# Moved steps in SyncE's queue and in a K block's reads: a graph layer and an attention layer on one core

## The chip, the cores and the metric

The kernel runs on one core of a Trainium2 chip. The metric is the device time of the whole kernel in microseconds (us). Before the change the median of three runs is 2260.26 us (2256.02 to 2264.42).

## The reference

The input x has 128 batch elements of 128 nodes with 512 features, in float32; adj is one 128x128 matrix for all of them.

```python
# layer 0
h = relu(layernorm(x))
x = x + norm_adj @ (h @ W0) + b0          # norm_adj = D^-1/2 adj D^-1/2
# layer 1: attention over the nodes, 8 heads of 64
h = relu(layernorm(x))
q, k, v = h @ Wq + bq, h @ Wk + bk, h @ Wv + bv
s = q k^T / sqrt(64) + (1 - adj) * -1e9
x = x + softmax(s) v @ Wo + bo
```

## The kernel before

**Tiles and stages.** The batch is cut into 32 groups of four elements (NG = 32, GB = 4). A group's x lies in SBUF as two tiles `xt`, half 0 (elements 0 and 1) and half 1 (elements 2 and 3), 512 KB each. The layers are pipelined over groups: in iteration t of the main loop the blocks run in the order W, Q, K, V, Y. W is the product with W0 for group t+1, Q, K and V are the projections for group t, Y is the output projection of group t-1. One iteration takes about 69 us.

**A projection** (class `Projection`) is one 512x512x512 product done as seven products of blocks P1 to P7, in the order P1, P5, P2, P6, P3, P7, P4, one for each step n = 0 to 6. P5, P2, P3 and P4 are again cut into seven products of smaller blocks each (`seven`, `phase`). TensorE writes them into PSUM banks: P1, P6, P7 in one of two banks a (they take turns between projections), P5 and P3 in d0 and d1, P2 in b, P4 in c. VectorE adds the pieces of a bank to the output tile (`add`, L440, and `read`, L455); the first read of each part is ScalarE's in Q, K and V. `step(n)` records the matmuls and the reads that go with them, `rest(n)` further reads of the same step. In K alone, `whole` is set: there P4 is computed in steps 4, 5 and 6 of its own block, ScalarE copies its first pieces (`part`, L768), and VectorE adds the others. In all other blocks the second and third phase of P4 are the `tail`, done in steps 1 and 2 of the next block.

In K's step 4, `rest` records seven reads: two of bank_d1 (`read_three`), one of bank_b, then four of bank_d0: `read_columns`, `read_across` column 0, `read_minus`, `read_across` column 1. Step 5 then records the read of bank_c that follows P4's second phase, and two of bank a. Step 6 writes P4's third phase into bank_c.

**Order.** Each engine runs its instructions in the order of the program. `plan` holds what else is put between the steps: `at(t, "W3", f, ...)` calls f before step 3 of block W of iteration t (with a letter b or c, after the step's first or second part). Within one slot the order is that of the calls of `at`. The program's order is then the order in each engine's queue. SyncE (SP) issues all DMAs, so an issue that has to wait holds up all that follow.

**What SyncE does around the change**, with g = t - 1 the group whose attention is being finished:
- `split_att(g, b)` (L848, L849): ScalarE splits element b's attention weights into two planes of 16 bits, and a DMA writes these to DRAM (`planes`).
- `turn_att(g, b)` (L852): a transposing DMA brings the planes back, transposed, into the tile `att`. `attend` (L874) then uses them at the start of V, in the order of elements 2, 3, 0, 1; in the program the results of 2 and 3 go to banks named `po`.
- `store_half(t - 2, 1)` (L892): the finished half 1 of group t - 2 goes out. Half 0 goes out at the end of the Y block before.
- `load_x(t + 2, (half,))` (L170): the x tiles of group t + 2. They take the buffers of group t - 2, so each load waits until the store of the same half has landed.
- `reload_w` (L1058): weights, in four parts per projection, from copies in DRAM (`wd_q` and so on) into two buffers in turn.

`ln1` (L325, L326, L330) takes the statistics of the new x on VectorE: half 0's first element in slot Q0b, its second in Q1b, half 1 in Q3b. The reads of W's tail from bank_c stand behind the first of these on VectorE.

Of the kernel before, what the change touches and what calls it, by code (L numbers as in the profile page):

```python
# [97 lines left out]
def kernel(  # L98
# [177 lines left out]


    INNER = [((T1, W22), step) for step in FIRST_RIGHT[:3]]
    INNER += [((W21, T4), WINOGRAD_RIGHT[0])]
    INNER += [((T1, W22), step) for step in FIRST_RIGHT[3:]]  # L280
    INNER += [((W21, T4), step) for step in WINOGRAD_RIGHT[1:]]

    def combine_inner(name, engine, steps=range(9)):
# [103 lines left out]
    class Projection:  # L387
# [110 lines left out]
        def read_phase(self, half, y, src, n, part=(0, 1)):  # L498
# [8 lines left out]
            else:  # L507
                self.add(dst[:, 1], m[:, 1:2].to_broadcast([P, 2, P]))

        def step(self, n):  # L510

            a, inner = bank[f"a{turn[0]}"], self.inner
            t, m = self.region(1, 0), bank["c"]
            left = tail.pop(0) if n in (1, 2) and tail else None
            if n == 0:
                self.left, self.right = self.a(), w_sb[self.w]
                self.product(a, P1, True)
                self.read_first(0, 0, a)
            elif n == 1:
                if inner:  # L520
                    self.seven(P5, True, (0,))
                else:
                    self.product(bank["d0"], P5, True)
                if left:
                    left[0]()
                if inner:
                    self.seven(P5, True, (1,))
            elif n == 2:
                if inner:
                    self.phase(bank["b"], P2, 0)  # L530
                else:
                    self.product(bank["b"], P2, True)
                if left:
                    left[0]()
            elif n == 3:
                self.product(a, P6, False)
                self.read_first(0, 1, a)
            elif n == 4:
                if inner:
                    self.phase(bank["b"], P2, 1)  # L540
                    if self.whole:
                        self.phase(m, P4, 0)
                    self.seven(P3, False, (1, 0))
                    self.read_phase(0, 0, bank["b"], 1, (0,))
                    if self.whole:

                        self.whole(t[:, 0, :], m[:, P : 3 * P], 0)
                        self.whole(t[:, 1, P:], m[:, 3 * P :], 1)
                        self.add(t[:, 0, :P], m[:, :P])
                else:  # L550
                    self.product(bank["d0"], P3, False)
            elif n == 5 and self.whole:
                self.phase(m, P4, 1)
                self.product(a, P7, False)
                self.whole(t[:, 1, :P], m[:, 3 * P :], 1)
                self.add(t[:, 1, :P], m[:, P : 2 * P])
                self.add(t[:, 0, :], a[:, : 2 * P])
                self.add(t[:, 1, P:], a[:, 3 * P :])
                turn[0] = 1 - turn[0]
            elif n == 5:  # L560
                self.product(a, P7, False)

                reads = [lambda: self.read_first(1, 0, a), lambda: self.read(1, 1, a)]
                for f in reads if self.stay else reads[::-1]:
                    f()
                turn[0] = 1 - turn[0]
            elif self.whole:
                self.phase(bank["b"], P2, 2)
                self.phase(m, P4, 2)
                self.read_phase(0, 0, bank["b"], 2)  # L570
                a = bank[f"a{1 - turn[0]}"]
                self.add(t[:, 1, :P], a[:, 2 * P : 3 * P])
                self.read(1, 1, a)
                self.read_phase(1, 0, m, 2)
            elif inner:
                self.phase(bank["b"], P2, 2)
                self.phase(bank["c"], P4, 0)
                self.read_phase(0, 0, bank["b"], 2)
                self.read_phase(1, 0, bank["c"], 0)
                for k in (1, 2):  # L580
                    tail.append(
                        (
                            lambda k=k: self.phase(bank["c"], P4, k),
                            lambda k=k: self.read_phase(1, 0, bank["c"], k),
                        )
                    )
            else:
                self.product(bank["c"], P4, True)
                self.read(1, 0, bank["c"])
            if n == 2:  # L590
                if inner:
                    self.read_phase(0, 0, bank["b"], 0)
                else:
                    self.read(0, 0, bank["b"])
            if left:
                left[1]()

        def rest(self, n):

            inner = self.inner  # L600
            if n == 1:
                if inner:
                    self.read_columns(1, 1, True)
                else:
                    self.read_first(1, 1, bank["d0"])
            elif n == 2 and inner:
                self.read_three(1, 1, 0)
                self.read_across(1, 1, 0)
                self.read_three(1, 1, 1)
                self.read_across(1, 1, 1)  # L610
                self.read_minus(1, 1)
            elif n == 4:
                if inner:
                    self.read_three(0, 1, 0)
                    self.read_phase(0, 0, bank["b"], 1, (1,))
                    self.read_three(0, 1, 1)
                    self.read_columns(0, 1)
                    self.read_across(0, 1, 0)
                    self.read_minus(0, 1)
                    self.read_across(0, 1, 1)  # L620
                else:
                    self.read(0, 1, bank["d0"])

# [170 lines left out]
    def turned_in_place(g, b):  # L794

        return g == NG - 1 or (g, b) in ((0, 2), (0, 3), (NG - 2, 3))
# [102 lines left out]
    def at(slot, place, f, *args):  # L899
        plan.setdefault((slot, place), []).append((f, *args))  # L900

    for t in range(-1, NG + 1):
# [3 lines left out]
        if 0 <= t - 1 < NG - 1:  # L906
            g = t - 1

            for first, final, place, f, *args in (
                ("W1", "-Y6", "Q0", turn_att, 0),  # L910
                ("W4b", "-Y6b", "W1b", split_att, 1),
                ("W5", "-Y3", "W2", exponentials, 2, 0, H // 2),
                ("W6", "-Y4", "W3", exponentials, 2, H // 2, H),
                ("Q0b", "-Y5b", "W4b", softmax_end, 2),
                ("Q1", "-Y5", "W5", exponentials, 3, 0, H // 2),
                ("Q2", "-Y6", "W6", exponentials, 3, H // 2, H),
                ("Q0", "Q1", "Q2", turn_att, 1),
                ("Q2b", "Q0b", "Q0b", softmax_end, 3),
                ("Q4b", "Q0b", "Q3b", split_att, 2),
                ("Q6b", "Q2", "Q5b", split_att, 3),  # L920
                ("K1", "Q2", "K0", turn_att, 2),
                ("K3", "Q5", "K2", turn_att, 3),
            ):
                place = first if t == 1 else final if last else place
                if f in (split_att, turn_att) and turned_in_place(g, args[0]):
                    continue
                at(t - place.startswith("-"), place.strip("-"), f, g, *args)
            if t == 1:
                at(1, "K3", transpose_att, g, 2)
                at(1, "K5", transpose_att, g, 3)  # L930
            elif last:
                at(t, "K1", transpose_att, g, 3)
            for b in (2, 3, 0, 1):
                at(t, "V0", attend, g, b)
# [35 lines left out]

            at(t, "Y3" if t == NG else "Q3" if last else "W3", store_half, t - 2, 1)
        if 3 <= t + 2 < NG:
            at(t, "W3" if t > 1 else "W0", load_x, t + 2, (0,))
            at(t, "W5" if t > 1 else "W0", load_x, t + 2, (1,))
        if 2 <= t + 2 < NG:
            g = t + 2
# [255 lines left out]
```

## Time and profile before

| what | value |
|---|---|
| median of three runs | 2260.26 us |
| profiled execution: its own time | 2266.76 us |
| its span | 2265.0 us |
| TensorE busy | 2231.4 us (99%) |
| VectorE busy | 1799.0 us (79%) |
| ScalarE busy | 1385.6 us (61%) |
| GpSimd busy | 1867.5 us (82%) |
| DMA, hardware queue of SyncE | 560.08 MB, 84.7% of 16 engines |
| granted TensorE clock | 0.999 |

The profile is one execution; its span runs from the first to the last instruction, and its own time lies some 6.5 us over the median of the runs. Times in a timeline are us from the start of the span: start, duration, engine, line, operation, tiles written and read, count; a number in brackets is the idle time of the engine just before, with what ended it. PE is TensorE, PEld its weight loads, DVE VectorE, ACT ScalarE, POOL GpSimd, SP SyncE, and a q behind a name its sequencer. A line of waits names who waited for whom, the total in us, the number of times and the longest. A DMA is told of twice: the time SyncE needs to issue it, and the time from issue to landing. L is the line in the kernel before.

### The profile page before, as it was taken

What the parts mean: (1) busy time and instruction counts of PE and PEld (TensorE: products, weight loads), DVE (VectorE), ACT (ScalarE), POOL (GpSimd) and SP (SyncE); (2) the same over time, 40 slices, a digit from 0 to 9 for tenths busy, and PEclk for the clock granted to TensorE, in tenths of its full rate; (3) what the DMA queues carried; (4) which work ended last, traced back from release to release, by engine and by line L of the source; (5) the groups of instructions that cost most, each with busy time, mean ns of one, the idle gap of its engine ahead of it and who ended that gap; (6) DMA issues with size and microseconds to landing.
All of it is one profiled execution on the core that took longest, in us unless ns stands there. A gap on an engine that the chain in (4) does not pass through costs nothing.

```text
span 2265.0 us, 79243 instructions
## 1 busy us (share of the span) xinstructions
PE 2231.4 (99%) x32679; PEld 1903.6 (84%) x32679; DVE 1799.0 (79%) x4371; ACT 1385.6 (61%) x3556; POOL 1867.5 (82%) x1928
## 2 busy tenths in 40 slices
PE   9999999999999999999999999999999999999999
PEld 7688888888888888888888888888888888888887
DVE  7778887877888778878778877788777887877876
ACT  4565665655666556666556665566665665655754
POOL 6899888888898888898888988888888888878864
PEclk9999999999999999999999999999999999999999
DMA  5478988899888899888898899998898988899982
GB/s 172 158 261 252 282 237 268 248 251 287 252 259 251 248 266 266 276 255 246 259 287 246 258 243 252 273 258 265 249 246 260 287 247 260 247 248 280 246 240 96
DMA packets 448697, 565.15 MB, mean 250 GB/s; under 512 B 326352, under 2 KB 333648, under 8 KB 447824
## 3 DMA queue, kind: packets, MB, share of 16 engines
q1 hardware_dynamic: 448336, 560.08, 84.7%
q8 instruction: 258, 4.23, 0.7%
q14 instruction: 103, 0.84, 0.1%
HBM read 358.68 MB, written 122.68 MB: 213 GB/s over the span
## 4 chain that ended last, share of the span: by engine, by line
PE 75%; DMA 13%; DVE 6%; SPq 2%; ACT 1%; issue 1%; POOL 1%; DVEq 0%; POOLq 0%
PE bank_a L140 27%; PE bank_d L140 16%; PE bank_b L140 9%; PE bank_c L140 8%; DMA xt<-in_x_dram 7%; PE pa L140 4%; DMA planes<-att 3%; DVE k L440 3%; PE bank_d L808 3%; PE po L874 2%; DMA att<-planes 2%; DVE xt L440 2%; SPq L852 2%; PE pt L725 1%; PE pss L808 1%; PE bank_b L874 1%
## 5 line engine op out<-in xcount | busy, mean ns | idle before, releaser
L835 ACT ACTIVATE att<-att,nmx 128x128 f32<-128x128 f32 x1024 | 396.4, 392 | 0.5 <-DMA w<-in_L_gnn_Wo_dram 0.5
L140 PE MATMUL bank_a<-op_h,w 128*64 128x256 f32 x2976 | 354.4, 380 | 0.0
L843 POOL TENSOR_TENSOR att<-att,rsm 128x1024 f32<-128x1024 f32 x128 | 242.0, 1900 | 48.4 <-DVE rsm L842 48.3
L440 DVE TENSOR_TENSOR xt<-xt,bank_d 128x512 f32<-128x512 f32 x610 | 269.4, 466 | 11.8 <-DVE xt L440 0.9
L140 PEld LDWEIGHTS bank_a<-op_h,w 128*64 128x64 f32 x2976 | 208.2, 137 | 81.9 <-issue 1.2
L344 ACT ACTIVATE h<-xt,nb,rs 128x512 f32<-128x512 f32 x254 | 207.3, 817 | 112.2 <-POOL nb L333 110.5
L848 ACT COPY att<-att 128x2048 uint16<-128x2048 uint16 x121 | 229.3, 1895 | 64.7 <-POOL att L843 64.7
L331 POOL TENSOR_TENSOR rs<-ve,mhalf 128x2 f32<-128x2 f32 (+1 forms) x129 | 92.0, 713 | 166.7 <-DVE ve L330 166.3
L140 PE MATMUL bank_d<-op_h,w 128*64 128x128 f32 (+1 forms) x3424 | 223.0, 275 | 0.9 <-DVE q L440 0.9
L325 DVE BATCH_NORM_STATS2 st<-xt 128x6 f32<-128x512 f32 x256 | 173.2, 676 | 58.6 <-DMA xt<-in_x_dram 58.6
L94 POOL TENSOR_TENSOR op_o<-op_o 128x256 f32<-128x256 f32 x297 | 210.9, 735 | 10.0
L94 POOL TENSOR_TENSOR op_a<-op_a 128x256 f32<-128x256 f32 x279 | 197.3, 732 | 12.8 <-DVE op_a L376 3.2
L140 PEld LDWEIGHTS bank_d<-op_h,w 128*64 128x64 f32 x3424 | 193.9, 137 | 12.6 <-DVE q L440 5.5
L94 POOL TENSOR_TENSOR op_h<-op_h 128x256 f32<-128x256 f32 x270 | 191.5, 734 | 12.4 <-DVE op_h L376 3.1
L765 ACT ACTIVATE q<-bank_a,bqk 128x256 f32<-128x256 f32 x192 | 80.0, 467 | 198.9 <-PE bank_a L140 198.9
L835 ACT ACTIVATION_READ_ACCUMULATOR att<-att,nmx 128x1 f32 x1024 | 195.4, 191 | 0.0
L140 PE MATMUL bank_a<-w,op_o 128*64 128x256 f32 x1536 | 182.2, 379 | 0.0
L140 PE MATMUL bank_a<-w,op_h 128*64 128x256 f32 x1488 | 177.9, 381 | 0.0
L140 PE MATMUL bank_a<-w,op_a 128*64 128x256 f32 x1488 | 176.4, 379 | 0.0
L455 DVE TENSOR_TENSOR xt<-bank_a,xt 128x512 f32<-128x512 f32 x252 | 166.5, 681 | 3.3 <-PE bank_a L140 2.9
L827 DVE TENSOR_REDUCE nmx<-att 128x8 f32<-128x1024 f32 x128 | 154.8, 1209 | 0.0
L348 POOL TENSOR_TENSOR xt<-xt,b 128x1024 f32<-128x1024 f32 (+1 forms) x65 | 153.1, 2358 | 0.0
(183 smaller groups left out, 5659.7 us busy)
## 6 DMA issues: line engine op xcount, KB each, us to landing
w<-wd_v SPq DMA_DIRECT2D x93, 704.0 KB, 5.9
w<-wd_o SPq DMA_DIRECT2D x93, 704.0 KB, 7.2
w<-wd_q SPq DMA_DIRECT2D x90, 704.0 KB, 6.7
planes<-att SPq DMA_DIRECT2D x121, 512.0 KB, 5.0
w<-wd SPq DMA_DIRECT2D x87, 704.0 KB, 5.9
xt<-in_x_dram SPq DMA_DIRECT2D x63, 512.0 KB, 6.7
out_dram<-xt SPq DMA_DIRECT2D x62, 512.0 KB, 4.9
planes_h<-att SPq DMA_DIRECT2D x29, 512.0 KB, 3.0
```

The lines of the kernel that those rows point to most:

```text
L94: engine.tensor_tensor(twice(out), twice(x), twice(y), ALU.subtract if minus else ALU.add)
L140: nc.tensor.matmul(out[y : y + P // 2], lhsT[:, y : y + P // 2], rhs, **flags)
L325: nc.vector.bn_stats(self.st[:, j, :], self.src[:, j, :])
L331: nc.gpsimd.tensor_tensor(self.rs[:, c], self.ve[:, c], mhalf[:, c], ALU.pow)
L344: nc.scalar.activation(h, src[:, j, :], AF.Relu, bias=nb[:, j : j + 1], scale=rs[:, j : j + 1])
L348: nc.gpsimd.tensor_tensor(t, t, bias.unsqueeze(1).to_broadcast([P, t.shape[1], D]), ALU.add)
L440: nc.vector.tensor_tensor(dst, dst, src, f)
L455: nc.vector.tensor_tensor(t, src.rearrange("p (r f) -> p r f", r=2), t, ALU.add)
L827: nc.vector.tensor_reduce(nmx, att_of(g, b), AX.X, ALU.max, negate=True)
L835: nc.scalar.activation(att[:, h, :], att[:, h, :], AF.Exp, bias=nmx[:, h : h + 1], scale=1.0, accum_out=sm[:, h : h + 1])
L843: nc.gpsimd.tensor_tensor(att, att, rsm.unsqueeze(2).to_broadcast([P, H, P]), ALU.mult)
L848: nc.scalar.copy(planes, halves)
```

## The change

Three steps move; nothing is added or taken out.

1. In K, three reads of the third product (P3, banks d0) leave `rest(4)`. They become `read_others` and are recorded in step 5, behind the read of P4's second phase from bank_c. Q, V, W and Y call `read_others` where the reads were.
2. `turn_att` of element 0 moves from slot Q0 to W5, that of element 1 from Q2 to Q0, in iterations 2 to 30. (In iteration 1 and in the last, other slots hold, which stay.) In W5 it is recorded ahead of the load of half 1.
3. `load_x` of half 0 moves from W3 to W2, ahead of the store of half 1 of group t - 2, in iterations 2 to 29.

SyncE's queue in such an iteration, before and after (the other issues keep their place):

```
before: planes 1, store half 1, x half 0, wd_q last, x half 1, wd_v 0, turn 0, wd_v 1, turn 1, planes 2, wd_v 2, planes 3, turn 2, turn 3
after:  planes 1, x half 0, store half 1, wd_q last, turn 0, x half 1, wd_v 0, turn 1, wd_v 1, planes 2, wd_v 2, planes 3, turn 2, turn 3
```

```diff
+        def read_others(self):
+            self.read_across(0, 1, 0)
+            self.read_minus(0, 1)
+            self.read_across(0, 1, 1)
...
                 self.whole(t[:, 1, :P], m[:, 3 * P :], 1)
                 self.add(t[:, 1, :P], m[:, P : 2 * P])
+                self.read_others()
                 self.add(t[:, 0, :], a[:, : 2 * P])
                 self.add(t[:, 1, P:], a[:, 3 * P :])
...
                     self.read_columns(0, 1)
-                    self.read_across(0, 1, 0)
-                    self.read_minus(0, 1)
-                    self.read_across(0, 1, 1)
+                    if not self.whole:
+                        self.read_others()
...
-                ("W1", "-Y6", "Q0", turn_att, 0),
+                ("W1", "-Y6", "W5", turn_att, 0),
...
-                ("Q0", "Q1", "Q2", turn_att, 1),
+                ("Q0", "Q1", "Q0", turn_att, 1),
...
-            at(t, "W3" if t > 1 else "W0", load_x, t + 2, (0,))
+            at(t, "W2" if t > 1 else "W0", load_x, t + 2, (0,))
             at(t, "W5" if t > 1 else "W0", load_x, t + 2, (1,))
```

## The prediction

> **What bounds the kernel now.** I read the page first (busy shares, then the chain that ended last), then the list of waits of the weight loads and of the matmuls, then the timelines of the engines around the waits that came out of it.
>
> ```profile
> PE 2231.4 (99%) x32679; PEld 1903.6 (84%) x32679; DVE 1799.0 (79%) x4371; ACT 1385.6 (61%) x3556; POOL 1867.5 (82%) x1928
> PE 75%; DMA 13%; DVE 6%; SPq 2%; ACT 1%; issue 1%; POOL 1%; DVEq 0%; POOLq 0%
> ```
>
> TensorE is busy 99% of 2265.0 us: whatever the change does, it can only take out waits of TensorE. The chain puts 13% on DMAs and 6% on VectorE, but it follows a wait back into work that ran beside the matmuls, so these shares are not what can be won. The waits are:
>
> ```profile
> PEld bank_c L140 <- DVE xt L440: 13.7, 19, 1.5
> PEld bank_c L140 <- DVE k L440: 9.5, 30, 0.3
> PEld po L874 <- POOL op_a L94: 9.0, 9, 1.8
> PEld bank_d L140 <- DVE q L440: 6.0, 25, 0.7
> ...
> PE po L874 <- DMA att<-planes: 7.1, 9, 1.6
> ```
>
> The columns are total us, times, longest. Four groups hold 38.2 us, 1.7% of the span. The third names GpSimd, but the matmuls of the same nine moments name the transposed attention tile: it is a DMA. One layer of the loop (t, about 69.7 us) shows where each arises.
>
> First, K. VectorE and ScalarE at the end of a K block:
>
> ```profile
> 1040.47 2.05 DVE L440 TENSOR_TENSOR k<-k,bank_d 128x256 f32<-128x256 f32 x5
> 1040.80 0.37 ACT L768 ACTIVATE k<-bank_c,bqk 128x128 f32<-128x128 f32 x1 [1.23 <-PE bank_c L140]
> 1042.44 0.28 DVE L440 TENSOR_TENSOR k<-k,bank_c 128x128 f32<-128x128 f32 x1
> 1042.78 0.20 PEld L140 LDWEIGHTS bank_c<-op_h,w 128*64 128x64 f32 x4 [0.32 <-DVE k L440]
> ```
>
> TensorE stands 0.32 us for the read of bank_c, which stands in VectorE's order behind five reads of bank_d that nobody awaits.
>
> Second, the x load. SyncE's queue and its reader, in the layer with a long wait:
>
> ```profile
> 1145.02 0.58 SPq L849 DMA_DIRECT2D planes<-att  x1
> 1147.97 0.39 SPq L892 DMA_DIRECT2D out_dram<-xt  x1
> 1148.46 0.69 SPq L170 DMA_DIRECT2D xt<-in_x_dram  x1
> 1149.23 0.82 SPq L1058 DMA_DIRECT2D w<-wd_q  x1
> 1156.38 0.37 SPq L170 DMA_DIRECT2D xt<-in_x_dram  x1
> 1156.80 0.46 SPq L1058 DMA_DIRECT2D w<-wd_v  x1
> 1157.31 4.83 SPq L852 DMA_TRANSPOSE att<-planes  x1
> ```
>
> ```profile
> 1157.55 0.69 DVE L325 BATCH_NORM_STATS2 st<-xt 128x6 f32<-128x512 f32 x1 [2.62 <-DMA xt<-in_x_dram]
> 1158.37 0.84 DVE L440 TENSOR_TENSOR xt<-xt,bank_c 128x256 f32<-128x256 f32 x2
> 1159.27 0.20 PEld L140 LDWEIGHTS bank_c<-w,op_a 128*64 128x64 f32 x4 [1.07 <-DVE xt L440]
> ```
>
> The landings, each read by asking for one DMA alone (issue to landing): the planes issued at 1145.0 took 10.0 us (landed 1155.0), the store of half 1 8.3 (1156.3), the x load of half 0 9.1 (1157.5), the last part of wd_q 9.4 (1158.6). They land in the order of issue, 1.1 to 1.3 us apart: this is a backlog, and place in the queue is arrival time. VectorE waits 2.62 us for x, the reads of bank_c stand behind its statistics, and TensorE waits 1.07 us. Then SyncE blocks from 1150.1 to 1156.3, until the store has landed whose buffer the second x load takes, and both transposing DMAs stand behind it.
>
> **What the Trainium skill says.** "DMA: Bandwidth & Descriptors", section "Queues, rings and completion order": a DMA's descriptors are taken in the order of the ring, and SP has one row of rings. The landings above agree. The same page, "Anatomy of one DMA — SWDGE (gpsimd) path": waits happen on the issuing sequencer, before the DMA is dispatched. This trace agrees: SyncE waited 150.4 us in 28 waits of L170 for stores to land. Prices from that page: 435 GB/s over the fabric ("Specifications"), so 512 KB is an estimated 1.2 us; the 1.1 to 1.3 us between landings agree.
>
> **The change part by part.** The instruction orders of both programs show that TensorE, ScalarE and GpSimd keep their order; only VectorE's K reads (31 blocks) and SyncE's queue (29 layers for the transposes, 28 for x) move. Nothing is added or removed.
>
> (a) K reads. Three reads of bank_d (two 128x128 and one 128x256, which start 0.73 us apart from first to the follower: 1041.71 to 1042.44) go behind the read of bank_c. That read then starts at 1041.71; ScalarE's part of the same tile, which it must follow, is done at 1041.17, so no new wait. It ends 0.73 us earlier; TensorE needs it 0.32 us earlier. Cover 0.41 us. The three moved reads end at 1042.7 and bank_d is next written by the scores at 1046.64. The reads of bank_a behind them keep their time. Gain: 30 x 0.32 = 9.5; I take 9, since a weight load has a little idle time of its own.
>
> (b) The x load of half 0, ahead of the store. Its buffer is that of the store issued at 1143.22, which took 4.0 us, so SyncE waits until 1147.2 and issues then, still inside the backlog. The store behind it is issued at its old time or up to 0.7 us later, and waits in the same backlog, as does wd_q's last part behind it, which the end of Q needs 8 us after it lands. So x lands in the store's old place: 1156.3 for 1157.5, 1.2 us earlier. It must not be counted more. The longest wait is 1.5 us, and few are over 1.2: of 13.7 us I let about 0.7 stay and take 13. The 25 waits of bank_d for q (0.18 each, 4.5 of the 6.0) come from the same late VectorE; I take 4.
>
> (c) The transposing DMA 0, ahead of the x load of half 1. It is issued at about 1150.1 in the time in which SyncE now blocks; its planes landed long ago. Its 4.8 us of issue end at 1155, before the store lands (now 1157.5). Its data go behind wd_q's last part (1158.6). Half 1 of x is then issued at 1157.5 instead of 1156.4, behind the transpose's 512 KB: 2.0 us at the 261 GB/s that the skill's page gives for a transposing DMA ("Latency and other measured facts"), and 1.6 by the trace, where the last two transposes of this layer land at 1178.5 and 1180.1. So x half 1 lands at about 1158.6 + 2.0 + 1.3 = 1161.9 for 1160.5. VectorE takes it at 1162.21 now and would be there at 1161.0: it waits 0.9 and is then 0.3 earlier than now, while TensorE is 1.07 earlier. The lag of 0.7 us is covered: VectorE's next idle time is 1.6 us (before bank_c of q), and its read of bank_b ends 1.8 us before that bank's next matmul. Cost 0, up to 1 us a layer if the transpose is slower. I put 1 us in all.
>
> (d) The transposes 0 and 1 leave SyncE's queue some 4 us earlier. Behind them stand the planes of batch elements 2 and 3 and their transposes. In the layer of the longest wait ScalarE had planes 3 ready at 1307.4, but SyncE issued them at 1309.7, being in transpose 1 until 1308.5; they landed 8.4 us later, transpose 3 at 1323.0, and the matmuls waited 1.6:
>
> ```profile
> 1302.66 5.84 SPq L852 DMA_TRANSPOSE att<-planes  x1
> ...
> 1309.70 0.89 SPq L849 DMA_DIRECT2D planes<-att  x1
> 1312.24 7.83 SPq L852 DMA_TRANSPOSE att<-planes  x2
> ```
>
> 2.3 us at the issue, and less data ahead of them (transpose 1 has landed by then), against a longest wait of 1.8: all nine go. 7.1 by the matmuls, 9.0 by the weight loads: I take 8.
>
> Weights: wd_v parts 0 and 1 are issued about 1 us later (1158 and 1163 for 1156.8 and 1162.2), and the V block that needs them begins near 1189. No wait there.
>
> Sum: 9 + 13 + 4 + 8 - 1 = 33 us. The profiled execution took 2266.8 us (span 2265.0), so 2233.8; the median of the runs is 2260.3, 6.5 below it, so 2227.
>
> **The rivals.** *x stays late* (half 0 is no earlier, or half 1 becomes what VectorE waits for): only (a) and (d) count, 2260 - 17 = 2243. For it: half 1 does land later. Against: 1.6 to 1.8 us of cover. *Transposes stay late*: planes 3 still waits for the DMAs, 2260 - 26 = 2234 or so, inside my range. *Waits only move on*, each to the next one in its layer: near 2255. Against: after each of the four the trace shows free time on the waited-for engine. *Slower*: transpose 0 in front of x half 1. The slowest transpose took 12.6 us to land; from 1150.1 this is 1162.7, and x follows at 1164. From about 1163.7 (now 1160.5) the cover is gone, and each us beyond costs 28 us, one per layer, while (b) brings nothing. 1.1 us beyond: 28 x 1.1 - 17 = +14, 2274. Against: transposes with little in front land within 4.7 to 7.7 us. That the change doesn't do what it says is excluded by the instruction orders.
>
> **How the numbers follow.** Forecast 0.63, transposes late 0.10, x late 0.18, waits move on 0.05, slower 0.04. A measurement of this kernel tells about 0.5% (11 us) from no change. Faster 0.91, same 0.05, slower 0.04. The floor is all 38 us and a few of what follows: 2218. The range goes from there to just over the x-late case, 2217 to 2245, and leaves out the last two cases, 0.09, and the edges of the others.
>
> **What would show it.** Right: no wait of bank_c for k; the x load of half 0 lands about 1.2 us before the store; bank_c's waits for xt under 2 us in sum; transpose 3 lands before po starts in every layer. Wrong: a new VectorE wait for the second x load of over 2 us, TensorE gaps at pa or bank_b in Q, or L892 pushed back by the load in front of it.

## The result, and the profile after

| what | before | after |
|---|---|---|
| median of six runs | 2261.36 us | 2240.27 us (2234.09 to 2244.95) |
| profiled execution: its own time | 2266.76 us | 2240.26 us |
| its span | 2265.0 us | 2238.5 us |

The ratio of the medians is 0.9906, with a 95% interval of 0.9886 to 0.9926: 21 us less, between 17 and 26. The forecast was 2227 with a range of 2217 to 2245: the sign and the range held, and the time is 13 us over the forecast. In the kernel after, lines from about L511 on stand 5 further down: 892 is L897, 852 is L857, 1058 is L1063.

The page of the kernel after, its busy shares and its chain by engine:

```profile
PE 2218.4 (99%) x32679; PEld 1905.3 (85%) x32679; DVE 1799.0 (80%) x4371; ACT 1387.1 (62%) x3556; POOL 1867.5 (83%) x1928
PE 89%; SPq 4%; DVE 2%; DMA 2%; POOL 2%; ACT 1%; issue 1%; POOLq 0%; DVEq 0%
```

The chain put 13% on DMAs before and puts 2% on them now, though the span went down by only 1.2%. That is why these shares were not taken for what can be won.

The list of waits of the kernel after (who waited for whom: total us, times, longest):

```profile
DVE st L325 <- DMA xt<-in_x_dram: 67.3, 51, 3.0
...
PEld bank_b L140 <- DVE q L440: 7.2, 9, 1.5
PEld pa L140 <- ACT h L344: 7.2, 23, 1.0
...
PE bank_b L140 <- DVE q L440: 4.9, 7, 1.2
```

The waits of bank_c for k and those of `po` are gone from the list. Those of bank_c for xt fell from 13.7 to 1.7 us, those of bank_d for q from 6.0 to 2.7, that of `pa` from 7.5 to 7.2. The first line for PEld is new: bank_b waits for q, 7.2 us in 9 layers. The sum by the weight loads is -9.5 - 9.0 - 12.0 - 3.3 - 0.3 + 7.2 = -26.9 us, close to the 26.5 by which the span fell. (All waits of weight loads together, the small ones included, fell from 70.2 to 40.1, so a match as close as this is partly chance.)

The end of a K block in the timeline of the kernel after:

```profile
1100.14 1.21 DVE L440 TENSOR_TENSOR k<-k,bank_d 128x256 f32<-128x256 f32 x2
1100.48 0.37 ACT L773 ACTIVATE k<-bank_c,bqk 128x128 f32<-128x128 f32 x1 [1.23 <-PE bank_c L140]
1101.27 0.28 DVE L440 TENSOR_TENSOR k<-k,bank_c 128x128 f32<-128x128 f32 x1
1101.46 0.81 DVE L440 TENSOR_TENSOR k<-k,bank_d 128x128 f32<-128x128 f32 x3
1102.10 0.25 PEld L140 LDWEIGHTS bank_c<-op_h,w 128*64 128x64 f32 x4
```

The read of bank_c starts behind two reads of bank_d instead of five, the three others follow it, and the weight load has no bracket: it waits for nothing. (The count x3 gives them one shape, since the view merges neighbours of one line.)

SyncE's queue in a layer of the kernel after with a long new wait:

```profile
1067.83 0.38 SPq L170 DMA_DIRECT2D xt<-in_x_dram  x1
1068.46 0.77 SPq L897 DMA_DIRECT2D out_dram<-xt  x1
1069.32 0.50 SPq L1063 DMA_DIRECT2D w<-wd_q  x1
1069.87 9.44 SPq L857 DMA_TRANSPOSE att<-planes  x1
1079.37 0.57 SPq L170 DMA_DIRECT2D xt<-in_x_dram  x1
1079.99 0.47 SPq L1063 DMA_DIRECT2D w<-wd_v  x1
1080.55 5.60 SPq L857 DMA_TRANSPOSE att<-planes  x1
```

And VectorE and TensorE in the same layer:

```profile
1084.64 0.69 DVE L325 BATCH_NORM_STATS2 st<-xt 128x6 f32<-128x512 f32 x1 [2.75 <-DMA xt<-in_x_dram]
...
1087.12 0.41 DVE L440 TENSOR_TENSOR q<-q,bank_b 128x256 f32<-128x256 f32 x1
1087.45 2.06 DVE L440 TENSOR_TENSOR q<-q,bank_d 128x256 f32<-128x256 f32 x5
1087.59 0.20 PEld L140 LDWEIGHTS bank_b<-op_h,w 128*64 128x64 f32 x4 [1.19 <-DVE q L440]
1087.59 0.44 PE L140 MATMUL bank_b<-op_h,w 128*64 128x128 f32 x4 [0.95 <-DVE q L440]
```

The landings of this layer: x half 0 at 1077.1, the store at 1078.4, the last part of wd_q at 1079.6, transpose 0 at 1083.5, x half 1 at 1084.6. So the place swap of step (b) is there, 1.3 us. But SyncE was still busy with the issue of transpose 0, 9.44 us long, when the store landed at 1078.4; the load that waited for that store was issued at 1079.4, and its data came behind the transpose's, which needed 3.9 us after wd_q's. VectorE waited 2.75 us for x half 1, and the matmuls into bank_b waited about 1 us for VectorE's late read.

Over the 28 layers of the loop (medians; issue and landing read from the trace for each):

| us | before | after |
|---|---|---|
| x half 0 lands, from the store's landing | +1.28 | -1.30 |
| issue of transpose 0 on SyncE | 5.5 | 8.3 (7.0 to 10.3) |
| that issue ends, from the landing of the DMA ahead | -0.13 | -0.20 |
| transpose 0 lands, after the DMA ahead of it | 1.9 | 3.25 |
| x half 1 issued, after the store's landing | 0.04 | 0.99 |
| x half 1 lands, after the store's landing | 4.1 | 5.6 |
| x half 1 lands, after half 0 | 2.7 | 6.95 |

Two of these rows need a closer look. The issue of transpose 0 has no fixed length: it ends with the landing of the DMA ahead of it, before and after. And the median of its landing hides two groups: under 2.1 us in 15 layers and over 3 us in 11 in the kernel before, 10 and 16 in the kernel after (2 lie between in each). Of the 9 layers in which bank_b waits, 7 are among these 16, with 6.0 of the 7.2 us.

### The profile page after: what moved, and what is told of

Its sections match the earlier page's. It is cut to its first block, busy times and chain, and to the rows that moved or that the text cites. A ratio compares the mean times of both kernels' runs of the same rounds, so it can differ in the third digit from the quotient of the medians.

```text
span 2238.5 us, 79241 instructions
## 1 busy us (share of the span) xinstructions
PE 2218.4 (99%) x32679; PEld 1905.3 (85%) x32679; DVE 1799.0 (80%) x4371; ACT 1387.1 (62%) x3556; POOL 1867.5 (83%) x1928
## 4 chain that ended last, share of the span: by engine, by line
PE 89%; SPq 4%; DVE 2%; DMA 2%; POOL 2%; ACT 1%; issue 1%; POOLq 0%; DVEq 0%
PE bank_a L140 33%; PE bank_d L140 20%; PE bank_b L140 10%; PE bank_c L140 10%; PE pa L140 4%; SPq L857 3%; PE bank_d L813 3%; PE po L879 2%; DMA xt<-in_x_dram 2%; PE pt L730 1%; PE pss L813 1%; PE bank_b L879 1%; PE bank_a L879 1%; PE bank_b L813 1%; DVE st L325 1%
## 5 line engine op out<-in xcount | busy, mean ns | idle before, releaser
L325 DVE BATCH_NORM_STATS2 st<-xt 128x6 f32<-128x512 f32 x256 | 173.2, 676 | 67.3 <-DMA xt<-in_x_dram 67.3
```

Source lines behind the costliest of these rows:

```text
L325: nc.vector.bn_stats(self.st[:, j, :], self.src[:, j, :])
```

## The experiments

Three theories stood after this. *Transpose theory*: transpose 0 ahead of x half 1 makes bank_b wait. *Store theory* (rival): the load of half 0 pushed the store back, and with it half 1, which waits for the store's landing; then bank_b would wait without the transposes too. *Scatter theory*, for the distance between the forecast and the median: the profiled execution of before had more of the waits than an average run has. The first four kernels do one part alone, or take wd_q's data out of the way.

**K alone.** The kernel after with both moves of the queue undone:

```diff
-                ("W1", "-Y6", "W5", turn_att, 0),
+                ("W1", "-Y6", "Q0", turn_att, 0),
-                ("Q0", "Q1", "Q0", turn_att, 1),
+                ("Q0", "Q1", "Q2", turn_att, 1),
-            at(t, "W2" if t > 1 else "W0", load_x, t + 2, (0,))
+            at(t, "W3" if t > 1 else "W0", load_x, t + 2, (0,))
```

> Of the kernel before, only the three reads of the third product in K are moved behind the read of bank_c. If the parts of the change add up, the waits of bank_c for k (9.5 us in 30) are gone and nothing else moves: 9 us off, about 2252. Rival (waits only move on): the 0.3 us per layer comes back at the x load or at po, because SyncE's queue does not move with TensorE: then 3 us or less off, and the waits of bank_c for xt or of po grow by 6 us.

Measured: 2253.72 us, ratio 0.9969 (0.9959 to 0.9979), 7.1 us less. In its trace the waits of bank_c for k are gone, those of bank_c for xt are 14.9 us (21 times), of `po` 6.2. The time from the last matmuls into bank_b to the first one into `po`, in which the wait lies, fell from 0.733 to 0.437 us in each of 30 blocks: 8.9 us. K's step stands by itself and does what was said.

**x half 0 alone.** The kernel before with only this line:

```diff
-            at(t, "W3" if t > 1 else "W0", load_x, t + 2, (0,))
+            at(t, "W2" if t > 1 else "W0", load_x, t + 2, (0,))
```

> Of the kernel before, only the x load of half 0 goes ahead of the store of half 1. My theory (the transposing DMA 0 in front of x half 1 makes the new waits of bank_b for q, 7.2 us in 9): here the transpose is still behind x half 1, so no wait of bank_b for q; bank_c's waits for xt fall from 13.7 to about 2; 14 us off, about 2247. Rival (the store, pushed back 1.3 us by the load in front of it, makes them, since x half 1 waits for the store): bank_b's waits for q are here too, 5 us or more, and only 8 us are off.

Measured: 2260.57 us, ratio 1.0003 (0.9991 to 1.0015): nothing, and the expected gain failed. The waits of the weight loads and matmuls of this kernel:

```profile
PEld po L874 <- POOL op_a L94: 12.7, 13, 1.8
PE po L874 <- DMA att<-planes: 10.8, 14, 2.0
...
PEld po L874 <- issue: 2.7, 3, 2.2
...
PEld po L874 <- PE bank_c L140: 2.1, 3, 1.0
...
PEld bank_c L140 <- DVE xt L440: 1.2, 2, 0.6
```

and SyncE's wait for the stores:

```profile
SPq L170 <- DMA out_dram<-xt: 239.7, 55, 9.0
```

The waits of bank_c for xt went from 13.7 to 1.2 us, as forecast, and those of `po` from 9.6 (9.0, and 0.6 named "issue") to 12.7 + 2.7 + 2.1 = 17.5. SyncE now waits 239.7 us for stores instead of 150.4, in 55 waits instead of 28. Of this, 38.7 us in 27 waits are those of the half 0 loads for the store of their own buffer, which are new; the 28 of half 1 grew from 150.4 to 200.9. The store stands one place further back and lands later; the load of half 1 waits for it, and the transposes stand behind that load. Counted from the layer's first matmul into `po`, that load is issued 1.2 to 1.4 us later than in the two executions of before (medians), transpose 0 lands 0.9 to 1.5 later and transpose 3 still 0.1 to 0.8. What was won at the start of the layer was paid back at its end. For the store theory this is the answer on the other point: x half 1 landed 3.7 us after the store here, and bank_b waited for q nowhere.

**The transposes alone.** The kernel before with only these lines:

```diff
-                ("W1", "-Y6", "Q0", turn_att, 0),
+                ("W1", "-Y6", "W5", turn_att, 0),
-                ("Q0", "Q1", "Q2", turn_att, 1),
+                ("Q0", "Q1", "Q0", turn_att, 1),
```

> Of the kernel before, only the transposing DMAs of elements 0 and 1 go forward; the x load of half 0 stays behind the store. My theory: po's waits (9.0) go; bank_c's waits for xt stay near 13.7; x half 1 is late behind the transpose here too, which adds up to 4 us at bank_b: 4 to 9 us off, about 2255. Rival (the store is what delays x half 1): it is at its old place here, so no wait of bank_b for q, 9 us off or a little more.

Measured: 2256.94 us, ratio 0.9982 (0.9974 to 0.9991), 4 us less. The waits of `po` are gone, the other waits stay (bank_c for xt 11.6, for k 9.6, bank_d for q 6.2). VectorE waits longer for x (78.8 us instead of 58.6), since x half 1 lands 6.9 us after the store. That is the transpose theory's lag, but the loss of up to 4 us that it expected at bank_b did not come: bank_b waits for q once, 0.7 us by the matmuls. Here half 0 is late too, so half 1 lands only 5.7 us after half 0, where it is 6.95 in the kernel after. The table of distances at the end of this section shows that the waits of bank_b go with this distance, not with the one from the store.

**The last part of wd_q behind x half 1.** The kernel after with the last part of the reload in Y's row moved:

```diff
-(t + 1, "W3" if t + 1 < NG - 1 else "Q5")
+(t + 1, "W5" if t + 1 < NG - 1 else "Q5")
```

> The changed kernel, with the last part of wd_q (448 KB) moved from ahead of the transposing DMA 0 to behind the x load of half 1. My theory (what lies in the queue ahead of x half 1 is its arrival time): the transpose and x half 1 land about 1.2 us earlier, VectorE's wait for the second load falls by that, bank_b's waits for q fall from 7.2 us to under 2, and 5 us more are off, about 2235. Rival (the store sets it): x half 1 lands as before, bank_b's waits stay at 6 us or more, 2240.

Measured: 2237.09 us, ratio 0.9899 (0.9879 to 0.9919). With wd_q's data behind it, x half 1 lands 4.5 us after the store instead of 5.6. The DMA ahead of transpose 0 is now the store itself, and the issue of the transpose ends 0.20 us before the store lands, so the load of half 1 goes out at once (0.02 us). No wait of bank_b for q is left, `po` waits 2.7 us in 4 layers, and the waits of `pa` for h stand at 9.3. So one us earlier is enough for bank_b. Beside the kernel after (0.9906, 0.9886 to 0.9926) the time is not told apart from it.

The next four: both moves of the queue without K, the order of transpose 0 and x half 1 turned round, transpose 0 taken out, and a dose of K's step.

**Both moves of the queue, without K's step** (the kernel before with the lines of the two experiments above):

> Of the kernel before, both edits of SyncE's queue together (x half 0 ahead of the store, transposes 0 and 1 forward), K's reads as they were. Alone, the first gave 0 us and the second 4. My theory (x half 0 alone pays its gain back at po, because the store behind it holds x half 1 and with it the transposes; with the transposes ahead of x half 1 that way back is closed): the two give more than their sum, 12 to 15 us off, about 2247, with po's waits at 0 and bank_c's waits for xt under 3 us. Rival (the parts add up): 4 us off, about 2256.

Measured: 2242.67 us against 2258.88 for before beside it, ratio 0.9928 (0.9914 to 0.9941): 16 us less, where the two moves alone gave 0 and 4. The parts do not add up: the load of half 0 loses at `po` what the transposes' earlier place then gives back. Its waits: bank_c for k 9.5, bank_b for q 2.4 in 4 layers, bank_d for q 1.7, `po` none.

**x half 1 first.** The kernel after with transpose 0 behind the load of half 1, in the same step:

```diff
-                ("W1", "-Y6", "W5", turn_att, 0),
+                ("W1", "-Y6", "W5b", turn_att, 0),
```

> The changed kernel, with the transposing DMA 0 behind the x load of half 1 instead of ahead of it. My theory: no wait of bank_b for q (7.2 us in the changed kernel), since the transpose's data no longer lie ahead of x; but the transposes start after the store has landed, and po's waits come back, 8 to 13 us: about 2250. Rival (it is the store, pushed back by x half 0, that makes x half 1 late): the waits of bank_b for q stay at 5 us or more.

Measured: 2241.45 us, ratio 0.9919 (0.9905 to 0.9934). SyncE in the same stretch of this kernel:

```profile
1070.71 0.38 SPq L170 DMA_DIRECT2D xt<-in_x_dram  x1
1071.53 0.39 SPq L897 DMA_DIRECT2D out_dram<-xt  x1
1072.01 0.63 SPq L1063 DMA_DIRECT2D w<-wd_q  x1
1081.46 0.37 SPq L170 DMA_DIRECT2D xt<-in_x_dram  x1
1081.88 3.52 SPq L857 DMA_TRANSPOSE att<-planes  x1
```

SyncE again stands idle from 1072.6 to 1081.5, for the store. The load goes out with its landing (0.02 us later, median), x half 1 lands 3.6 us after the store, and bank_b waits for q nowhere: the store theory is refuted, the transpose in front is the cause. In return `po` waits 5.0 us in 10 layers, less than the 8 to 13 that were expected, and the time is not told apart from the kernel after: the place in front of half 1 won nothing that shows in the medians. The transpose's issue took 3.0 us (median) instead of 8.3, and again ended with the landing of the DMA ahead, here x half 1 (0.17 us before it).

**Without transpose 0** in iterations 2 to 30 (element 0's attention weights stay untransposed there):

```diff
+                if f is turn_att and args[0] == 0 and t > 1 and not last:
+                    continue
```

> The changed kernel without the transposing DMA of element 0 in iterations 2 to 30: attention of these elements is computed with weights that are not transposed. It measures what the transpose costs x half 1 where it stands. My theory: SyncE is free when the store lands, x half 1 lands about 3 us earlier than in the changed kernel, VectorE's waits for x fall from 67 to about 25 us, bank_b's waits for q go, 6 us off the changed kernel, about 2234. Rival (DMA bandwidth over the layer is the limit): with 512 KB less read and written each layer, more than 15 us go, at other waits too.

Measured: 2230.71 us, ratio 0.9876 (0.9858 to 0.9893), against 0.9906 for the kernel after: about 7 us less by the ratios, and 10.3 us less in the span (2228.2 for 2238.5; 7.2 against the second execution of after below). It is about what the waits of bank_b hold (7.2 and 4.9) and a little more: VectorE's waits for x fell from 67.3 to 20.3 us, and the waits of bank_c for xt (1.7) are gone; bank_d for q keeps 1.7. So 7 to 10 us is what the transpose costs in that place. That no better place could win more is argued, since its data are gone from the queue too.

**One of K's three reads.** The kernel after with only the last of the three moved:

```diff
-                self.read_others()
+                self.read_across(0, 1, 1)
...
-                    if not self.whole:
+                    if self.whole:
+                        self.read_across(0, 1, 0)
+                        self.read_minus(0, 1)
+                    else:
                         self.read_others()
```

> The changed kernel, but of the three reads in K only the last (128x128) goes behind the read of bank_c. If TensorE's wait is VectorE's order alone, the read of bank_c is 0.19 us earlier than before instead of 0.73, the wait is 0.32 - 0.19 = 0.13 us, 30 times, 4 us in all: about 4 us slower than the changed kernel, 2244. Rival (ScalarE's copy sets it): no wait is left with one read already, 2240.

Measured: 2238.08 us, ratio 0.9907 (0.9892 to 0.9922), not told apart from the kernel after; the 2244 did not come, and by the time alone the rival (no wait left) would stand. In its trace the time from bank_b to `po` is 0.536 us, between 0.733 (none moved) and 0.437 (all three): 0.10 us, 3 us over 30 blocks, is left, a little under the 0.13 us that was expected. So the order of VectorE's reads sets this wait, as the expectation said; a dose as small as this is below what the medians tell, and the trace alone shows it.

The last three ask how much one execution differs from another of the same kernel.

**Before once more.**

> The kernel before once more, for a second profile beside the two below on one chip. The first profile was of an execution 6 us over the median. My theory for the part of the forecast that did not come: those 6 us were waits of bank_c for xt and of po that an average execution does not have, so a profile of an execution near 2260 has 6 us less in these two groups (22.7 in the first), and the same 9.5 for k. Rival: the groups hold as much as in the first profile, and the difference lies elsewhere.

Measured: 2258.26 us, ratio 1.0002 (0.9992 to 1.0012); the profiled execution took 2262.6 us, 4.1 less than the first. Its waits:

```profile
PEld bank_c L140 <- DVE xt L440: 14.2, 18, 2.3
PEld bank_c L140 <- DVE k L440: 9.7, 30, 0.3
...
PEld bank_d L140 <- DVE q L440: 5.4, 24, 0.7
...
PEld po L874 <- POOL op_a L94: 4.5, 4, 1.5
```

Those of `po` are half of the first execution's (4.5 for 9.0, 4 layers for 9), and that is about the difference of the two spans (4.2 us). Those of bank_c for xt are as large as before: this part of the scatter theory fell.

**After once more.**

> The changed kernel once more. If the waits of bank_b for q (7.2 us in the first profile) vary between executions as the kernel without the K edit (2.4) suggests, they are 2 to 7 us here, and the span differs from the first (2238.5) by the same. About 2240.

Measured: 2236.23 us, ratio 0.9902 (0.9889 to 0.9914); span 2235.4. bank_b waits 4.9 us for q in 7 layers, so the new wait was there again, smaller.

**wd_q behind, once more**, beside it:

> The changed kernel with the last part of wd_q behind the x load of half 1, beside the changed kernel on the same chip. My theory: 3 to 5 us less than the changed kernel, with no wait of bank_b for q. Rival: the same time within the noise, what is won at bank_b being lost at po.

Measured: 2236.37 us, ratio 0.9898 (0.9884 to 0.9912); no wait of bank_b for q, but `po` 4.2 us in 6 layers. What is won at bank_b is lost at `po`, and this version is not told apart from the kernel after. No better version came out of the experiments.

TensorE's lost time in the traces, worked out by adding up how much later each matmul started after the one two before it than this pair of forms usually does, tells the same story (us over the span, good to some 3 us, by what is taken as usual):

| kernel | lost |
|---|---|
| before, before once more | 52.5, 48.8 |
| x half 0 alone | 49.1 |
| transposes alone | 41.3 |
| K alone | 40.1 |
| both moves of the queue, without K | 26.8 |
| after, after once more | 26.7, 23.6 |
| x half 1 first | 24.2 |
| one of K's reads | 23.5 |
| wd_q behind, once more | 22.0, 23.4 |
| without transpose 0 | 14.9 |

And how far half 1 of x landed behind half 0 (median of 28 layers), with the layers in which the weight loads of bank_b waited for q:

| kernel | us | layers |
|---|---|---|
| before, before once more | 2.7, 2.9 | 0, 0 |
| K alone | 2.7 | 0 |
| x half 1 first | 4.9 | 0 |
| without transpose 0 | 4.9 | 0 |
| x half 0 alone | 5.0 | 0 |
| transposes alone | 5.7 | 0 |
| wd_q behind, once more | 5.9, 5.8 | 0, 0 |
| both moves of the queue, without K | 6.9 | 4 |
| after, after once more | 6.95, 6.97 | 9, 7 |
| one of K's reads | 6.96 | 6 |

In each of these 26 layers the distance is 6.9 us or more (though about two in three layers with such a distance do not wait). Half 0 sets when VectorE gets to the reads of bank_c, half 1 how long it is then held up before those of bank_b; the change moves the one forward and the other back.

## Why the prediction was right, and where it missed

**(a) K's reads: right.** 9 us forecast, 9.5 of listed wait gone, 8.9 by the distance from bank_b to `po`, and 7.1 by the medians of K alone.

**(b) The load of half 0: right in the mechanism, with something left out.** The 1.2 us of earlier arrival were 1.3, and 17 us of waits forecast to go were 12.0 + 3.3 = 15.3. What the step did not see: alone the move is worth nothing. Step (c) had the store land a whole place later (1157.5 for 1156.3) and half 1 issued behind it, but asked only what this does to half 1. In the kernel before, the transposes stand behind that load, and they are held back with it. The forecast of (b) came out because the change moves the transposes too.

**(c) Transpose 0 in front of x half 1: the term that was mis-sized.** It stood at 1 us and cost 7.2 by the first profile (4.9 in the second, 2.4 without K's step). The lag was named, and so was the cover of 1.6 to 1.8 us. By the sum, half 1 came 4.4 us after the store and 5.6 after half 0 (1161.9 for 1156.3); it came 5.6 and 6.95 after.

What failed in the sum is the time of the transpose's data. It was put at 2.0 us, the price of 261 GB/s that the Trainium skill gives ("DMA: Bandwidth & Descriptors", "Latency and other measured facts": measured on one kernel, for a non-contiguous middle dimension), and held against the last two transposes of one layer. The data landed 3.25 us after the DMA ahead (median), 1.25 more, and that is nearly the whole difference. The price fits the layers of the faster group alone, and the slower group was in the trace of before as well, in 11 of 28 layers. The cover was sized nearly right: the rival "slower" has it end at 1163.7, which is 7.4 us after half 0, and the waits came from 6.9 on. So this rival came in a small dose, in 9 of the 28 layers, and with it the sign of being wrong that the prediction named: VectorE's waits of over 2 us for half 1, and gaps at bank_b.

A second duration was wrong, but cost nothing. The issue was put at 4.8 us, from a layer in which the transpose stood elsewhere in the queue. That length was the time until the DMA ahead of it, wd_v's first part, landed (issue ended at 1162.14, landing at 1162.38). In the new place the DMA ahead is wd_q's last part, and by the prediction's own figure for that (1158.6) SyncE would come free about 1 us after the store's landing; the load went out 0.99 us after it. But half 1 landed 1.2 to 1.4 us behind the transpose (medians) in every kernel that has it behind, whether its load was issued 0.02 us after the store (wd_q behind), 0.99 (after) or 2.3 (transposes alone).

**(d) The transposes leave earlier: right.** 8 us forecast, and the 9.0 of `po` are gone in every layer.

**From the profile to the median: the other half of the miss.** By the profiled executions the forecast was 2266.8 - 33 = 2233.8, and 2240.3 came: 6.5 us, which is step (c) and the small differences of the others (33 forecast, 26.5 measured). Then 6.5 us more were taken off for the distance of the profiled execution from the median. In the kernel after that distance is 0.0 us (2240.26 and 2240.27), and in its second execution 0.9; in the second execution of before it was 4.4 (2262.6 for 2258.3). If the excess of the first profile of before was itself made of waits, the sum had already removed it, and to subtract it as well counted it twice. Shown of this are the 4.5 us of `po` by which the two executions of before differ; that the rest of the 6.5 is of the same kind is argued.

**The rivals.** That the range held owes something to its upper end, which was drawn just over the rival *x stays late* (2243). This rival lies nearest to the time, but the mechanism is not its own: half 0 was early, and the waits for it went. *Transposes stay late* did not happen. *Waits only move on* did, in part and in one place, from bank_c for xt to bank_b for q, and fully in the kernel with x half 0 alone.

**Left open:** why the landings of the transposes fall into two groups. It is not chance from run to run: the two executions of after have 24 of their 28 layers in the same group. Nor is the longer queue shown as the cause, since the kernel with x half 0 alone, where transpose 0 stands in its old place, has a median of 3.34 us. No run was aimed at it. Open, too, is why the issue ends when the DMA ahead lands; that it waits for room in the queue would fit, but no run shows it.

## What to carry to other kernels

A queue in which issues wait is a chain: before a load is put ahead of a store, ask which later issue waits for that store's landing, and what stands behind it. Read a duration in all layers before it goes into a sum: one layer, or a median over two groups, hides the slower ones, and the cover has to hold for these. Ask of an issue time what ends it, since that may be another DMA, which changes with the place. Where a profiled execution lies above the median, part of the excess can be the very waits that are to go (here 4.5 us of `po`): taking off both the waits and the distance can count them twice.

## What the runs showed of the hardware

- The issue of the transposing DMA 0 (512 KB) held SyncE for 3.0 us in the median behind x half 1, 5.5 in the kernel before, and 8.3 (up to 10.3) in the kernel after. In all twelve traces that have it, the issue ended with the landing of the DMA ahead of it: the medians are 0.13 to 0.23 us before that landing. When another DMA was put ahead of it (wd_q behind), the end moved with it. While it was issued, SyncE issued no other DMA.
- The data of transpose 0 landed after the DMA ahead of them in two groups, under 2.1 us and over 3 us, in every kernel that has it: 15 and 11 of the 28 layers before, 10 and 16 after, 15 and 5 with x half 1 first (8 lay between).
- Single runs of the kernel before went from 2252.8 to 2268.8 us (49 runs). `po`, which waits for the last of a chain of DMAs, waited 4.5 us in one execution and 9.0 in another; bank_c's wait for k, which VectorE's order sets, was 9.5 and 9.7.
